# Two convolution layers with weights made per position: pairs of positions as a 128-row stationary operand, the weights of four outputs in one moving pass, and the small networks moved beside the statistics

## The chip, the cores and the metric

The kernel runs on one core of one Trainium2 chip. The metric is the device time of one execution in microseconds (us). Every time below is a median of several executions on the chip, measured in turns with the kernel before on the same chip; a profiled execution of the same kernel is read beside it. One core gives no neighbours on its die to compare with; all profiled runs told here were classed as fast.

## The reference, cut to what matters

The input x has 32 samples (S), 32 batch entries (B), 64 channels (C) and 256 positions (L), all fp32. Two layers of the same form follow each other:

```python
h  = relu(ln(z @ W1 + b1))                        # per (b, l): 16 -> 128
w  = (h @ W2 + b2).reshape(B, L, CI, CO, K)       # own 64 x 64 x 3 weights for every (b, l)
hb = relu(ln(z @ Wb1 + bb1)); bias = hb @ Wb2 + bb2
x_uf = stack of x shifted by -1, 0, +1            # K = 3 taps along l
out  = einsum('sbilk,bliok->sbol', x_uf, w) + bias
x = x + conv(group_norm(x))                       # 32 groups of 8 positions
```

So every position of every batch entry has its own three 64 x 64 matrices, made by a matmul from 128 hidden values, and used for 32 samples only. Making the weights costs more TensorE time than using them.

## The kernel before

Both kernels go through 64 steps (32 batch entries, two layers) of two chunks. In a chunk the weights of 128 positions are made into an SBUF tile `wall` (through PSUM and VectorE, which adds the bias b2); then the convolution of the chunk before is done from `wall`. In the kernel before, the upper and the lower 64 partitions hold the two halves of the positions, so the stationary operands of the weight matmuls are 64 columns wide, and two of them stand in the array side by side (those of the convolution are 64 rows by 32 columns):

```python
def make_weights(t, w2, hT, c, kk, tick):          # once per tap kk
    for o0 in range(0, C, OG):                     # 8 groups of 8 outputs
        pg = ps_g.tile([P, OG, NP], FP, tag="pg", name="pg")
        for o in range(OG):
            for r in range(2):                     # the two halves of the positions
                nc.tensor.matmul(pg[r*C : r*C+C, o, :], w2[k][:, o0+o, :], h[:, r, :, c, :], ...)
        nc.vector.tensor_tensor(wall[...], pg..., b2..., ALU.add)
        tick()                                     # one piece of prepare(b + 1)

def convolve(xn, c):                               # K = 64 rows, two row halves x four column quarters
    for m in range(-1, LC + 1):
        ...
        nc.tensor.matmul(pc[r][q][t*S : (t+1)*S, ...], xn[r*C : (r+1)*C, t*LT + c*LC + m + 1, :], moved(...), ...)

def prepare(par, t, b, res):                       # the small networks of the next batch entry,
    for net in ("w", "b"):                         # spread over the groups of make_weights
        ... matmul, ScalarE, matmul (mean), ScalarE, matmul (variance), ScalarE ...
        nc.vector.reciprocal(sd, sd)               # L255
        nc.vector.tensor_tensor(hc, hc, sd, ALU.mult)   # L256
```

## Time and profile before

The time before was 6762.27 us (median of 3 runs, 6744.58 to 6773.44).

| | before |
|---|---|
| span of the profiled run | 6806.9 us |
| first dense weight matmuls | 412 us |
| one step of the loop | 99.7 us |
| TensorE stops at instruction fetches | 979 us |
| granted clock in the loop | 0.87 |

The prediction shows the main lines. Three more of the page of the kernel before are of use: the granted clock in 40 slices (tenths of full speed), the queue that moves instructions (packets, megabytes, share of the engines' time), and the chain that ended last by engine.

```profile
PEclk9999888898888888898888888888888888988888
...
q8 instruction: 1096, 17.96, 1.3%
...
PE 65%; issue 15%; DVE 8%; DMA 7%; SPq 5%; ACT 1%; POOL 0%; DVEq 0%; POOLq 0%; ACTq 0%
```

The clock stays below full speed all through the loop, and 15% of the chain is "issue", that is TensorE waiting for nothing that the profile shows, which the prediction reads as instruction fetches.

Two stretches of the same kernel, the statistics stage and the loop of layer 0, by engine: length, busy time (and instructions) of PE, PEld, DVE, ACT and POOL, then the clock, the DMA share and GB/s.

```profile
60.00:400.00 340.00, 15.17 (x26) 4.80 (x26) 174.52 (x493) 8.34 (x16) 9.54 (x7) 1.00 0.90 195
520.00:3440.00 2920.00, 2106.19 (x64262) 1931.26 (x64266) 1475.92 (x1994) 148.37 (x326) 810.85 (x208) 0.87 0.59 88
```

In the statistics stage TensorE and ScalarE are nearly empty, and the DMA engines are at 90%. That room is what the change wants to use.

### The profile page before, as it was taken

What the parts mean: (1) busy time and instruction counts of PE and PEld (TensorE: products, weight loads), DVE (VectorE), ACT (ScalarE), POOL (GpSimd) and SP (SyncE); (2) the same over time, 40 slices, a digit from 0 to 9 for tenths busy, and PEclk for the clock granted to TensorE, in tenths of its full rate; (3) what the DMA queues carried; (4) which work ended last, traced back from release to release, by engine and by line L of the source; (5) the groups of instructions that cost most, each with busy time, mean ns of one, the idle gap of its engine ahead of it and who ended that gap; (6) DMA issues with size and microseconds to landing.
All of it is one profiled execution on the core that took longest, in us unless ns stands there. A gap on an engine that the chain in (4) does not pass through costs nothing.

```text
span 6806.9 us, 289596 instructions
## 1 busy us (share of the span) xinstructions
PE 4626.3 (68%) x140322; PEld 4231.2 (62%) x140322; DVE 3263.5 (48%) x4649; ACT 332.3 (5%) x725; POOL 1735.7 (25%) x462
## 2 busy tenths in 40 slices
PE   0057767777766777676677667767776676777667
PEld 0046666666666766676666666766666666766666
DVE  4455445454544555454455444445444444545444
ACT  0000000000000000000001000000000000000000
POOL 0033322322322232233203322223223223222320
PEclk9999888898888888898888888888888888988888
DMA  9947565565656546655745655655654655656564
GB/s 193 226 84 110 76 102 87 77 92 90 93 74 102 88 74 95 90 90 76 102 86 87 109 83 82 95 84 87 88 93 71 96 90 76 91 91 93 71 101 54
DMA packets 2651853, 637.58 MB, mean 94 GB/s; under 512 B 2122240, under 2 KB 2647872, under 8 KB 2647872
## 3 DMA queue, kind: packets, MB, share of 16 engines
q1 hardware_dynamic: 2650688, 619.05, 59.2%
q8 instruction: 1096, 17.96, 1.3%
q14 instruction: 69, 0.57, 0.0%
HBM read 350.53 MB, written 268.44 MB: 91 GB/s over the span
## 4 chain that ended last, share of the span: by engine, by line
PE 65%; issue 15%; DVE 8%; DMA 7%; SPq 5%; ACT 1%; POOL 0%; DVEq 0%; POOLq 0%; ACTq 0%
PE pg L340 47%; PE pc L367 13%; SPq L330 5%; DMA xs<-in_x_dram 4%; DVE hc L256 3%; DVE hsd L255 3%; DMA zt<-in_L_conv_z_dram 2%; PE p L242 2%; PE p L250 1%; PE p L236 1%; DVE wall L343 1%; DMA w<-in_L_conv_W_dram 1%; PE p L265 1%; ACT hTb L259 1%; DVE y L382 0%
## 5 line engine op out<-in xcount | busy, mean ns | idle before, releaser
L340 PE MATMUL pg<-hTw,w 128*64 128x64 f32 x98304 | 3440.0, 236 | 651.7 <-issue 527.0
L340 PEld LDWEIGHTS pg<-hTw,w 128*64 128x64 f32 x98304 | 3307.4, 151 | 872.6 <-issue 686.3
L343 DVE TENSOR_TENSOR wall<-pg,b 128x512 f32<-128x512 f32 x3072 | 2104.0, 690 | 2282.8 <-PE pg L340 2277.5
L367 PE MATMUL pc<-wall,xn 64*32 64x192 f32 (+2 forms) x40960 | 898.0, 314 | 452.7 <-issue 451.5
L367 PEld LDWEIGHTS pc<-wall,xn 64*32 64x32 f32 x40960 | 772.8, 113 | 561.8 <-issue 526.1
L305 POOL TENSOR_TENSOR xn<-xt,gmean 128x4096 f32<-128x4096 f32 x64 | 474.1, 7408 | 2434.8 <-PE pc L367 2270.7
L382 DVE TENSOR_TENSOR y<-pc,y 128x512 f32<-128x512 f32 x512 | 339.7, 684 | 993.8 <-PE pc L367 990.2
L313 POOL TENSOR_TENSOR xt<-xt,bias 128x4096 f32<-128x4096 f32 x64 | 524.5, 8195 | 1096.5 <-ACT bias L267 1096.5
L305 POOL TENSOR_TENSOR xn<-xn,rstd 128x4096 f32<-128x4096 f32 x64 | 663.7, 10371 | 5.0
L236 PE MATMUL p<-zt,W 16*128 16x256 f32 x128 | 55.6, 520 | 399.4 <-DMA zt<-in_L_conv_z_dram 398.1
L236 PEld LDWEIGHTS p<-zt,W 16*128 16x128 f32 x128 | 23.3, 225 | 406.5 <-issue 400.7
L169 DVE BATCH_NORM_STATS2 parts<-xs 128x6 f32<-128x256 f32 x512 | 168.6, 408 | 197.5 <-DMA xs<-in_x_dram 150.2
L256 DVE TENSOR_TENSOR hc<-hc,hsd 128x256 f32<-128x256 f32 x128 | 251.4, 1964 | 4.4
L175 PE MATMUL am_ps<-am,quarter 128*128 128x32 f32 x2 | 0.6, 411 | 371.8 <-DVE am L126 371.8
L238 ACT ACTIVATE hh<-p,b 128x256 f32<-128x256 f32 x64 | 30.3, 474 | 4379.7 <-PE p L236 4379.7
L293 POOL MEMSET xt<- 64x32 f32 x64 | 9.7, 151 | 878.3 <-DMA xb<-xt 878.3
L175 PEld LDWEIGHTS am_ps<-am,quarter 128*128 128x128 f32 x2 | 0.5, 313 | 371.8 <-DVE am L126 371.8
L255 DVE RECIPROCAL hsd<-hsd 128x256 f32<-128x256 f32 x128 | 223.0, 1743 | 14.2 <-ACT hsd L252 14.2
L265 PE MATMUL p<-hTb,Wb 128*64 128x128 f32 x256 | 40.8, 414 | 242.5 <-ACT hTb L259 242.5
L384 DVE BATCH_NORM_STATS2 between<-y 128x6 f32<-128x512 f32 x256 | 177.8, 694 | 8.7
L265 PEld LDWEIGHTS p<-hTb,Wb 128*64 128x64 f32 x256 | 17.4, 187 | 252.5 <-ACT hTb L259 252.5
L242 PE MATMUL p<-hh,center 128*128 128x256 f32 x256 | 115.1, 540 | 2.3 <-ACT hh L238 2.3
(60 smaller groups left out, 673.6 us busy)
## 6 DMA issues: line engine op xcount, KB each, us to landing
xb<-xt SPq DMA_DIRECT2D x128, 1024.0 KB, 10.9
y<-xb SPq DMA_DIRECT2D x512, 256.0 KB, 6.4
xt<-in_x_dram SPq DMA_DIRECT2D x64, 1032.0 KB, 14.4
xt<-x SPq DMA_DIRECT2D x64, 1032.0 KB, 14.4
xs<-in_x_dram SPq DMA_DIRECT2D x64, 1024.0 KB, 40.1
x<-y SPq DMA_DIRECT2D x256, 256.0 KB, 8.0
out_dram<-y SPq DMA_DIRECT2D x256, 256.0 KB, 7.9
w<-in_L_conv_W_dram SPq DMA_DIRECT2D x6, 2048.0 KB, 24.7
```

What stands on the lines that cost most here:

```text
L169: nc.vector.bn_stats(parts[:, g, 2 * q + h, :], t[:, :, g * E : (g + 1) * E])
L242: nc.tensor.matmul(p2, center, h, start=True, stop=True)
L255: nc.vector.reciprocal(sd, sd)
L256: nc.vector.tensor_tensor(hc, hc, sd, ALU.mult)
L305: nc.gpsimd.tensor_tensor(o, i, st[:, :, 1 : GH + 1, None].to_broadcast(shape), op)
L313: nc.gpsimd.tensor_tensor(i, i, bias[:, None, :].to_broadcast([P, S, H]), ALU.add)
L330: nc.sync.dma_start(out=to[:, b, :, l0 : l0 + LT], in_=y[t * S : (t + 1) * S, r])
L340: nc.tensor.matmul(pg[r * C : r * C + C, o, :], w2[k][:, o0 + o, :], h[:, r, :, c, :], start=True, stop=True)
L343: nc.vector.tensor_tensor(wall[:, kk + c, :, o0 : o0 + OG], pg.rearrange("p o l -> p l o"), t["b2"][:, k, None, o0 : o0 + OG].to_broadcast ...
L367: nc.tensor.matmul(pc[r][q][t * S : (t + 1) * S, n0 - q * E : n1 - q * E, :], xn[r * C : (r + 1) * C, t * LT + c * LC + m + 1, :], moved(r ...
L382: nc.vector.tensor_tensor(part, pc[r][q].rearrange("p n o -> p o n"), part, ALU.add)
L384: nc.vector.bn_stats(between[:, r, g, b, :], part)
```

## The change

The intent is to need fewer TensorE instructions in the loop and to take the small networks out of it. Positions are handled in pairs (2p, 2p+1), so the 128 rows of the convolution's stationary operand are 64 channels at two neighbouring positions, and the weights of up to four neighbouring output positions (4 x 64 = 256 columns) move past it. Three kinds of weight groups feed this: kinds 0 and 1 make two taps at once with a 128-column stationary operand, kind 2 makes the two outer taps with two 64-column operands. The small networks run for two batch entries at a time beside the first statistics, and their results wait in DRAM (`hd`, `bd`) until a step loads them. The core of the diff:

```diff
-        for o in range(OG):
-            for r in range(2):
-                nc.tensor.matmul(pg[r * C : r * C + C, o, :], w2[k][:, o0 + o, :], h[:, r, :, c, :], ...)
+            for k in range(OG):
+                w = w2[:, og * OG + k, :]
+                if kind == 0:
+                    nc.tensor.matmul(pg[:, k, :], w[:, C : K * C], even, start=True, stop=True)
+                elif kind == 1:
+                    nc.tensor.matmul(pg[:, k, :], w[:, 0 : 2 * C], odd, start=True, stop=True)
+                else:
+                    nc.tensor.matmul(pg[0:C, k, :], w[:, 2 * C : K * C], odd, start=True, stop=True)
+                    nc.tensor.matmul(pg[C:P, k, :], w[:, 0:C], even, start=True, stop=True)
 ...
-                    for r in range(2):
-                        nc.tensor.matmul(pc[r][q][...], xn[r * C : (r + 1) * C, ...], moved(r, t, c, m, n0, n1), ...)
+                        nc.tensor.matmul(pc[t * S : (t + 1) * S, ...], xn[c][:, t, p + 1, :],
+                                         wall[:, t, a : a + (n1 - n0) * C], ...)
 ...
-    def prepare(par, t, b, res):            # in the loop
+    def hidden(stage, zts, small, i):       # beside first_stats, results to hd[i], bd[i]
 ...
+        def load_pairs(u):
+            src = (x[:, u] if u < B else x1[u - B]).rearrange("s c l -> c s l")
+            nc.sync.dma_start(out=xt[0:C], in_=src)
+            nc.sync.dma_start(out=xt[C:P, :, 0 : L - 1], in_=src[:, :, 1:L])
 ...
+        def after(u, c):                    # after the convolution of (u, c)
+            if u + 1 < U and u + 1 != B:
+                normalize(c)
+            if c == NCH - 1:
+                store(u)
+                ...
+                if u + 2 < U:
+                    load_pairs(u + 2)
+                    load_residual(u + 2)
+                    add_bias(u + 2)         # four pieces through one buffer
 ...
+        order = [(2, og) for og in range(NO)] + [(kind, og) for og in range(NO) for kind in range(2)]
```

## The prediction

> **What bounds the kernel now.** I read the page's busy line first, then the costliest groups, the waits, the chain in order of time, and last the start times of single TensorE records. The main loop has 64 steps (32 batches, two layers), each of two chunks.
>
> ```profile
> PE 4626.3 (68%) x140322; PEld 4231.2 (62%) x140322; DVE 3263.5 (48%) x4649; ACT 332.3 (5%) x725; POOL 1735.7 (25%) x462
> ...
> L340 PE MATMUL pg<-hTw,w 128*64 128x64 f32 x98304 | 3440.0, 236 | 651.7 <-issue 527.0
> ...
> L343 DVE TENSOR_TENSOR wall<-pg,b 128x512 f32<-128x512 f32 x3072 | 2104.0, 690 | 2282.8 <-PE pg L340 2277.5
> L367 PE MATMUL pc<-wall,xn 64*32 64x192 f32 (+2 forms) x40960 | 898.0, 314 | 452.7 <-issue 451.5
> ```
>
> No engine is full. VectorE waits for TensorE (2277.5 us at the weights, 990.2 us at L382), so TensorE's queue sets the pace. An fp32 matmul is two records, each with its weight load: 98304 is twice 128 chunks x 24 groups x 16 matmuls. What stops TensorE is seen in the chain:
>
> ```profile
> 2064.43 3.95 PE pg L340 x128
> 2068.38 0.35 issue
> 2068.72 3.95 PE pg L340 x128
> 2072.67 0.34 issue
> 2073.01 3.95 PE pg L340 x128
> 2076.96 0.34 issue
> 2077.31 3.95 PE pg L340 x128
> 2081.26 4.46 issue
> ```
>
> Every 128 records (256 instructions counting weight loads) it stops without a wait. The instruction queue moved 17.96 MB in 1096 packets of 16,384 bytes; 17.96 MB over 280,644 TensorE instructions is 64 bytes each, and a packet is 256. So these are instruction fetches. In the DMA records a packet takes 1.3 us on average, and TensorE resumes some 1.4 us after it landed. The two "issue" sums, 527.0 + 451.5 = 979 us, are 0.9 us a fetch.
>
> Second, the small networks sit in TensorE's queue and wait for ScalarE and VectorE:
>
> ```profile
> 400.43 0.54 DVE L256 TENSOR_TENSOR hc<-hc,hsd 128x256 f32<-128x256 f32 x1
> 404.39 1.75 DVE L255 RECIPROCAL hsd<-hsd 128x256 f32<-128x256 f32 x1 [3.43 <-ACT hsd L252]
> 406.18 5.17 DVE L256 TENSOR_TENSOR hc<-hc,hsd 128x256 f32<-128x256 f32 x1
> ```
>
> The same multiplication took 0.54 us and, beside a GpSimd operation, 5.17 us. Third, the granted clock is 0.87 in the main loop: these idle stretches cost clock too.
>
> The dense pace is read from the first groups:
>
> ```profile
> 418.73 0.69 DVE L343 TENSOR_TENSOR wall<-pg,b 128x512 f32<-128x512 f32 x1 [0.24 <-PE pg L340]
> 419.66 0.69 DVE L343 TENSOR_TENSOR wall<-pg,b 128x512 f32<-128x512 f32 x1 [0.24 <-PE pg L340]
> 420.59 0.69 DVE L343 TENSOR_TENSOR wall<-pg,b 128x512 f32<-128x512 f32 x1 [0.24 <-PE pg L340]
> ```
>
> A group of 16 matmuls takes 0.93 us: 32 records, two column halves at once, so 58.4 ns per pass of each half. In dense convolution stretches a record takes 20 ns (16 per 0.32 us): 192 columns x 0.83 ns / 8 array tiles. Per step: 48 x 0.93 + 2 x 320 x 0.020 = 57 us. The stretch from 520 to 3440 us holds 64262 records at 2194 a step, so a step lasts 99.7 us. Over 40 us per step are small networks, stops and half clock.
>
> **What the Trainium skill says.** "TensorE: Matmul & The Clock Gate", section "LDWEIGHTS (loading the stationary operand)", gives columns / 1.2 ns whatever the rows. The trace agrees: at L242 (128 stationary columns) the second load starts 107 ns after the first, at L340 (64 columns) 54 ns. At L242 the second matmul starts 320 ns after the first, 107 + 213: a load overlaps the preceding matmul, and 256 moving columns take 213 ns a pass. Same page, "Part 1: The HAM clock gate": half or full clock, decided over windows of 3413 ns. The clock records are 0.5 or 1.0 in multiples of 3.413 us. I summed the array work per window (columns x 0.83 ns x share of the array): all 1309 windows with at least 0.40 of a full array were followed by full clock, all 432 below 0.30 by half; between, about half each. "SBUF — State Buffer", "Who interferes with whom", says a VectorE instruction with two SBUF inputs contends with GpSimd; 0.54 against 5.17 us fits.
>
> **The change, part by part**, per chunk (half a step).
>
> Weights, full-width kinds 0 and 1: 8 groups x 16 matmuls, 128 stationary columns, 64 moving. The moving side takes 53 ns, but the load 107 ns, and a full-width load has no other column half to run beside. With the 5 ns by which 58.4 exceeds 53.3, a pass is 112 ns: 256 x 0.112 = 28.6 us. Before, 16 of the 24 groups made these for 14.9 us. The halved matmul count does not pay; the weight load becomes the bound.
>
> Kind 2 (two half-width matmuls, as before): 4 groups x 32 matmuls x 2 passes x 58.4 / 2 = 7.5 us. Weights together: 36.1 against 22.4 us.
>
> Convolution: 4 quarters x 4 tiles x 1024 columns x 2 passes x 0.833 / 4 column tiles = 6.8 us against 6.4. A quarter of the streamed blocks are zeros, and the row halves no longer run as two tiles.
>
> Fetches: 352 matmuls x 4 = 1408 instructions, 5.5 fetches against 8.5. In kinds 0 and 1, 256 instructions last 14 us; the fetch starts some 100 instructions ahead (1.4 us before the stop, median, at 14.6 ns each), 5.6 us there, which covers it. The two in kind 2 at 1.0 and 1.5 in the convolution at 0.5 us leave 2.8 us against 7.6.
>
> VectorE: 16 operations of 1024 elements at 157 + 1024 x 1.04 = 1.22 us (0.69 for 512, scaled), 19.5 us, plus 4 x 0.68 and, in layer 0, 4 x 0.69: 25 us. It lies under TensorE except after a convolution, where kind 2 needs 2.44 us of VectorE for 1.87 of TensorE and three buffers: about 0.8 us of wait. Changes of shape, some 0.25 us each (seen at 2087): 0.8 us.
>
> Sum: 28.6 + 7.5 + 6.8 + 2.8 + 0.8 + 0.8 = 47.3 us a chunk, x 128 = 6055 us. Before: 49.9.
>
> Small networks beside the statistics: L255 and L256 (474 us of VectorE) and TensorE's waits leave the loop. The statistics stage: 512 x 0.41 = 209 us, 32 hidden blocks x 1.4 = 45, merges about 40, first loads 25, a tail of 10: some 330 us to the first dense weights, against 412. It becomes VectorE-bound, because 4 MB in one piece should beat the 209 GB/s of today's loads. Layer change and end: 35 us. Total 6055 + 330 + 35 = 6420 us. The base holds no half clock; I leave it there because unforeseen savings (shorter stops) and losses look equal in the middle, and put the half clock in the tail.
>
> GpSimd per step: 16 x 1.3 + 28 x 0.34 + 4 x 2.3 = 40 us (2 ns an element over 0.28, from L313 and L306), hidden. Transfers: 10.1 MB a step, but in pieces of 256 B to 4 KB for 128 to 516 B. The chain normalisation, pair load, residual, four bias pieces, next hidden block is about 70 us of the 85 available.
>
> **Rivals.** (1) Half clock. Kinds 0 and 1 fill 53/112 = 0.48 of a window, above the 0.40 seen to suffice, but a stop that drops it would be self-sustaining: at half clock L242's loads lie 164 ns apart, so the work is 0.32, where 23 of 27 half-clock windows stayed half. If it catches one chunk in eight, +15 us each, 6660; if always, some 8300. For: the thin margin. Against: nothing waits within that stretch. (2) Load and matmul do not overlap in a full-width stream: 160 ns a pass, 59.6 us a chunk, 8000 us. Against: L242's 320 ns. (3) The in-order DMA queue becomes the bound: hidden blocks stand behind four bias pieces through one buffer, each waiting for GpSimd. At 20 us late a step, +1280 us, 7700. Against: the 15 us of slack and half as many pieces. (4) Fetches hide altogether: 2.8 us less a chunk, 6060.
>
> **Range and chances.** The two sides nearly cancel in the loop (47.3 against 49.9), so 2 us a chunk, 256 us, decides. Base within some 300 us; (1) at one eighth of the chunks or more has perhaps 0.15, (2) and (3) together 0.1, (4) 0.1. So 6420 us, 6050 to 7150, faster by over 2% (below 6627) 0.68, within 0.12, slower 0.20.
>
> **What would show it.** Kinds 0 and 1: VectorE's full-height evacuations every 3.6 us, 112 ns between passes; 5.1 us would be (2), under 2.5 us my load argument wrong. Granted clock above 0.95 in the loop, and no fetch stops in kinds 0 and 1; a clock near 0.7 would be (1). A wait of the weight matmuls on the hidden block's DMA would be (3). First dense weights at about 330 us. TensorE records 90,000, fetches about 720.

## The result, and the profile after

The changed kernel took 6834.9 us (median of 4 runs, 6814.48 to 6852.78) where the kernel before took 6767.15 us (4 runs). Ratios here and below are the mean time of one kernel's fast runs over that of the other's of the same rounds, so not quite the ratio of the medians: 1.0105, with a 95% interval of 1.0068 to 1.0143. By the 2% criterion that is the same. 6420 us and a gain had been predicted.

The lines of the page of the changed kernel that answer to those of before: busy time, clock, instruction queue, chain, and four costly groups (busy time and mean of one in ns; then idle time before them).

```profile
PE 6225.5 (91%) x91016; PEld 5820.7 (85%) x91016; DVE 3272.1 (48%) x3512; ACT 191.6 (3%) x757; POOL 2455.1 (36%) x3082
...
PEclk7567999999898889999999998999999899999999
...
q8 instruction: 713, 11.68, 0.8%
...
PE 86%; issue 5%; DVE 4%; DMA 2%; ACT 2%; POOL 1%; SPq 1%; ACTq 0%; DVEq 0%; POOLq 0%
...
L400 DVE TENSOR_TENSOR wall<-pg,b 64x1024 f32<-64x1024 f32 (+1 forms) x2048 | 2503.7, 1223 | 2345.3 <-PE pg L385 1215.2
L383 PE MATMUL pg<-hT,w2t 128*128 128x64 f32 x16384 | 2005.9, 283 | 24.0 <-DVE wall L400 15.8
...
L416 PE MATMUL pc<-wall,xn 128*32 128x192 f32 (+2 forms) x24576 | 1022.8, 325 | 240.1 <-issue 212.3
```

TensorE went from 140322 records to 91016, and yet its busy time rose from 4626 to 6226 us. It is now the bound in earnest: 91% busy, and idle "issue" time is down from 15% to 5% of the chain. Fewer instructions and fewer fetches (713 packets for 1096) came as intended; what remained of the work is longer. In the first four slices the clock is at 0.5 to 0.7, where the kernel before had 0.9.

The statistics stage and the loop of layer 0, in the same columns as before:

```profile
60.00:460.00 400.00, 261.83 (x841) 182.86 (x841) 218.79 (x622) 175.14 (x706) 0.00 (x0) 0.57 0.50 186
520.00:3440.00 2920.00, 2719.98 (x40485) 2572.49 (x40478) 1436.32 (x1381) 0.00 (x0) 1114.41 (x1390) 0.92 0.59 107
```

In the stage no engine is full: VectorE works 219 of 400 us, the transfers no longer fill the engines (0.50), and TensorE runs at half clock.

In the loop, kinds 0 and 1 are as dense as predicted. The chain in order of time (start, length, what) in a quiet stretch:

```profile
2925.92 3.57 PE pg L385 x32
2929.50 3.57 PE pg L383 x32
2933.07 3.57 PE pg L385 x32
2936.64 3.57 PE pg L383 x32
```

A pass is one TensorE record, and an fp32 matmul is two. 32 passes take 3.57 us, 111.6 ns each, with no stop in hundreds of instructions. Elsewhere the same groups take twice as long:

```profile
1840.85 3.36 issue
...
1847.04 7.02 PE pg L383 x32
1854.06 6.83 PE pg L385 x32
1860.89 6.83 PE pg L383 x32
```

A stop of 3.36 us in kind 2 dropped the clock to half at 1843.4 us, and it stayed there for 61.4 us, until the chunk's full-width groups were over: 6.83 us for 32 passes is 213 ns each. Seven spells of 51 to 65 us like this one, after stops of 1.1 to 4.8 us, hold nearly all the slow passes of kinds 0 and 1. And the convolution stops for long stretches at a time when blocks of x are being loaded. First the chain, then SyncE's queue of DMA issues (start, length of the issue, what) in the same stretch:

```profile
3092.08 4.79 PE pc L416 x104
3096.87 3.35 issue
3100.21 2.77 PE pc L416 x24
```

```profile
3070.06 0.60 SPq L114 DMA_DIRECT2D xt<-in_x_dram  x1
3070.71 2.76 SPq L115 DMA_DIRECT2D xt<-in_x_dram  x1
3073.59 28.80 SPq L338 DMA_DIRECT2D ys<-in_x_dram  x4
```

The pair load is issued at 3070 us and the residual pieces until 3102 us; the stop of 3.35 us at 3096.87 us lies in between, at the end of the pair load (its second half lands 24.9 us after its issue) and beside the residual pieces.

From the start times of all TensorE records, sorted by kind, the loop splits like this (us in all, 128 chunks). A stop is a long gap between two starts.

| | predicted | after | of it: stops | passes at half clock |
|---|---|---|---|---|
| statistics stage, to the first dense weights | 330 | 472 | | |
| kinds 0 and 1 | 28.6 x 128 = 3661 | 3857 | 4 | 1749 of 32768 |
| kind 2, with its fetch stops and waits | (7.5 + 2.0 + 0.8) x 128 = 1318 | 1215 | 189 | 1865 of 32768 |
| convolution, with its fetch stops and changes of shape | (6.8 + 0.75 + 0.8) x 128 = 1069 | 1273 | 308 | 2182 of 24576 |

The 0.75 is one and a half fetches at 0.5 us. Of the 308 us of stops in the convolution, 46 are two waits at the start of the loop and at the change of layer, 235 are 73 fetch stops of 3.2 us each, and the rest are short gaps at half clock. Of the 189 us in kind 2, some 120 are fetch stops (the page's "issue" at its two lines, 66.8 and 51.3 us); the rest are short waits where the shape changes or VectorE is late. The loop, change of layer included, is 6346 us where 6055 was predicted. With the stage 142 us late, and 17 us after the loop where 35 had been allowed for end and change of layer, that is the whole error of 415 us.

### The profile page after: what moved, and what is told of

Its sections match the earlier page's. It is cut to its first block, busy times and chain, and to the rows that moved or that the text cites. A ratio compares the mean times of both kernels' runs of the same rounds, so it can differ in the third digit from the quotient of the medians.

```text
span 6835.0 us, 194215 instructions
## 1 busy us (share of the span) xinstructions
PE 6225.5 (91%) x91016; PEld 5820.7 (85%) x91016; DVE 3272.1 (48%) x3512; ACT 191.6 (3%) x757; POOL 2455.1 (36%) x3082
## 4 chain that ended last, share of the span: by engine, by line
PE 86%; issue 5%; DVE 4%; DMA 2%; ACT 2%; POOL 1%; SPq 1%; ACTq 0%; DVEq 0%; POOLq 0%
PE pg L383 28%; PE pg L385 28%; PE pc L416 15%; PE pg L387 10%; PE pg L388 3%; DVE wall L400 2%; PE p L166 2%; ACT junk L152 1%; PE p L147 1%; DMA hd<-ht 1%; DVE hs L157 1%; POOL xn L374 0%; DVE ys L426 0%; DMA xt<-in_x_dram 0%; DVE between L428 0%
## 5 line engine op out<-in xcount | busy, mean ns | idle before, releaser
L400 DVE TENSOR_TENSOR wall<-pg,b 64x1024 f32<-64x1024 f32 (+1 forms) x2048 | 2503.7, 1223 | 2345.3 <-PE pg L385 1215.2
L383 PE MATMUL pg<-hT,w2t 128*128 128x64 f32 x16384 | 2005.9, 283 | 24.0 <-DVE wall L400 15.8
L385 PE MATMUL pg<-hT,w2t 128*128 128x64 f32 x16384 | 2005.3, 283 | 0.0
L383 PEld LDWEIGHTS pg<-hT,w2t 128*128 128x128 f32 x16384 | 1958.0, 199 | 36.2 <-PE pg L388 27.5
L385 PEld LDWEIGHTS pg<-hT,w2t 128*128 128x128 f32 x16384 | 1962.6, 200 | 0.0
L352 POOL TENSOR_TENSOR ys<-ys,bt 128x1024 f32<-128x1024 f32 x256 | 602.2, 2353 | 3448.6 <-DMA bt<-bd 2990.2
L416 PE MATMUL pc<-wall,xn 128*32 128x192 f32 (+2 forms) x24576 | 1022.8, 325 | 240.1 <-issue 212.3
L416 PEld LDWEIGHTS pc<-wall,xn 128*32 128x32 f32 x24576 | 742.3, 115 | 507.9 <-issue 250.6
L387 PE MATMUL pg<-hT,w2t 128*64 128x64 f32 x16384 | 1078.6, 228 | 76.8 <-issue 66.8
L388 PE MATMUL pg<-hT,w2t 128*64 128x64 f32 x16384 | 1079.2, 228 | 51.5 <-issue 51.3
L374 POOL TENSOR_TENSOR xn<-xt,gmean 128x32 f32<-128x32 f32 (+1 forms) x1408 | 1024.8, 728 | 262.5 <-PE pc L416 211.9
L387 PEld LDWEIGHTS pg<-hT,w2t 128*64 128x64 f32 x16384 | 1027.6, 143 | 103.1 <-issue 73.8
L388 PEld LDWEIGHTS pg<-hT,w2t 128*64 128x64 f32 x16384 | 1028.2, 143 | 64.6 <-issue 64.3
L374 POOL TENSOR_TENSOR xn<-xn,rstd 128x32 f32<-128x32 f32 (+1 forms) x1408 | 879.5, 625 | 111.7 <-ACT rstd L317 1.5
## 6 DMA issues: line engine op xcount, KB each, us to landing
xt<-in_x_dram SPq DMA_DIRECT2D x32, 2048.0 KB, 14.5
ys<-x SPq DMA_DIRECT2D x128, 512.0 KB, 14.5
xt<-in_x_dram SPq DMA_DIRECT2D x32, 2040.0 KB, 24.9
```

The source lines that it names most:

```text
L352: nc.gpsimd.tensor_tensor(y[:, oq, :], y[:, oq, :], bt, ALU.add)
L374: nc.gpsimd.tensor_tensor(o, i, b, op)
L383: nc.tensor.matmul(pg[:, k, :], w[:, C : K * C], even, start=True, stop=True)
L385: nc.tensor.matmul(pg[:, k, :], w[:, 0 : 2 * C], odd, start=True, stop=True)
L387: nc.tensor.matmul(pg[0:C, k, :], w[:, 2 * C : K * C], odd, start=True, stop=True)
L388: nc.tensor.matmul(pg[C:P, k, :], w[:, 0:C], even, start=True, stop=True)
```

## The experiments

Fifteen kernels ran on the chip after the change, in four groups; those of one group shared the runs of the kernel before. Each is an edit of the changed kernel. All gave correct results except four, which leave out or freeze transfers. The theory at the start: kinds 0 and 1 lose by their weight load (112 ns for what two half-width passes side by side do in 58.4 ns); the loop of normalisation, pair load and bias pieces stands close behind TensorE; the half clock is kept alive by the full-width groups themselves; and the fetch stops are long where transfers run. The rivals are named in each expectation.

| run | us, median | ratio to before, 95% interval |
|---|---|---|
| the change | 6834.9 | 1.0105 (1.0068 to 1.0143) |
| half | 6626.65 | 0.9755 (0.9720 to 0.9791) |
| unchain | 6656.16 | 0.9747 (0.9665 to 0.9828) |
| half_unchain | 6015.66 | 0.8860 (0.8827 to 0.8892) |
| pre | 6812.13 | 1.0010 (0.9945 to 1.0075) |
| mix_unchain | 6245.7 | 0.9201 (0.9184 to 0.9218) |
| quiet (wrong) | 4770.14 | 0.7029 (0.7015 to 0.7044) |
| hybrid | 5963.37 | 0.8786 (0.8765 to 0.8807) |
| half_mix_pre2 | 5860.7 | 0.8631 (0.8603 to 0.8659) |
| mix_only | 6689.18 | 0.9838 (0.9798 to 0.9878) |
| hybrid_mix | 6023.68 | 0.8847 (0.8819 to 0.8875) |
| hybrid_mix_al | 6017.49 | 0.8848 (0.8824 to 0.8871) |
| half_mix_al | 5887.53 | 0.8645 (0.8608 to 0.8682) |
| after_quiet (wrong) | 6237.67 | 0.9180 (0.9145 to 0.9215) |
| after_nopairs (wrong) | 6252.96 | 0.9205 (0.9185 to 0.9224) |
| after_nobias (wrong) | 6680.2 | 0.9827 (0.9793 to 0.9860) |

### half: kinds 0 and 1 at half width

```diff
-   nc.tensor.matmul(pg[:, k, :], w[:, C : K * C], even, ...)
+   nc.tensor.matmul(pg[0:C, k, :], w[:, C : 2 * C], even, ...)
+   nc.tensor.matmul(pg[C:P, k, :], w[:, 2 * C : K * C], even, ...)
```

and the same for kind 1 with `odd`.

> One edit to the changed kernel: in kinds 0 and 1 each full-width matmul is two half-width ones into the two column halves, same weights, same outputs. Theory (the full-width weight load binds, 112 ns a pass): a group falls from 3.6 to 1.9 us, the 28.7 us of kinds 0 and 1 to about 15 us a chunk, so TensorE alone would need about 37 us a chunk and the run would last about 5250 us. Second theory, to be told apart by the same run (a loop of GpSimd and the DMA queue lies just beneath: two normalisations 30 us, pair and residual loads 32, four bias pieces 32 = 94 to 97 us a step in the trace of the changed kernel, against 99 on TensorE): the step stops at 95 us, the run lasts about 6600 us, and TensorE now waits for the hidden block or for the normalised input. If the load does not bind: no change or slower (more instructions), 6800 us or more.

It took 6627 us. Among the waits of this kernel a new one stands out (engine, line, what it waited for: us in all, times, longest):

```profile
PE pg L389 <- DMA hT<-hd: 628.0, 63, 21.4
```

TensorE now waits 10 us a step for the next hidden block, which stands in SyncE's queue behind four bias pieces that pass through one buffer. The step is 95.9 us (loop 6140 us over 64 steps). That is the second of the two expectations. In the changed kernel the pair loads follow each other at 93 to 97 us in most steps, but TensorE's own steps there are as long, so this interval does not say which of the two sets it, and TensorE waited for the hidden block only once, for 1.8 us; its mean step of 99.2 us (6346 over 64) comes from a few steps of 112 to 127 us. What shows the second bound is half itself: with some 1600 us less for TensorE to do (4648 us busy for 6226), the step shrank only to 95.9 us, some 3 us a step. So the weights alone could not show their gain.

### unchain: the bias pieces and the hidden block elsewhere

```diff
-   bp = ctx.enter_context(tc.tile_pool(name="bias", bufs=1))
+   bp = ctx.enter_context(tc.tile_pool(name="bias", bufs=2))
     normalize(c)
+    if c == 0 and 1 <= u and u + 1 < U:
+        add_bias(u + 1)
 ...
                     load_residual(u + 2)
-                    add_bias(u + 2)
 ...
-   if c == 1 and u + 1 < U:
+   if c == 0 and u + 1 < U:
         hs[u + 1] = load_hidden(u + 1)
```

> Full-width weights as in the changed kernel; only the loop of GpSimd and the DMA queue is shortened: the bias of the next step is added after the first normalisation instead of before it, with two bias buffers, and the hidden block is loaded one chunk earlier. If TensorE binds alone: same as the changed kernel, 6835 us within 1.5 percent, though the fetch stops may move since the transfers move. If the loop already held TensorE back: faster by 2 percent or more.

It took 6656 us. The gain is not that of a wait for the queue, for the changed kernel hardly had one: the loads fall into another part of the step, and the convolution went from 1273 to 973 us. Kinds 0 and 1 gave 197 us back: 3515 of their passes ran at half clock for 1749 before (4054 for 3857 us). Four of the long slow spells followed stops in kind 2, and eleven followed stops of 0.9 to 3.2 us within the first 50 passes of the full-width stretch: the fetches there are not covered in every place of the loads.

### half_unchain: both

> Both edits. If the weight load binds first and the loop second: about 75 to 80 us a step (TensorE 37 to 40 us a chunk with 7.5 fetches in place of 5.5, the loop about 70), 5300 to 5650 us, and VectorE at over 60 percent. If the loop was no bound: same as the half-width run alone.

It took 6016 us, a gain of 11% over the kernel before, but not the 5300 to 5650 that the dense pace promised. Kinds 0 and 1 held 456 stops of 2.3 us, 1033 us in all: at half width a group has twice the matmuls, so twice the instructions in half the time, and the fetches that full-width groups cover stand bare again. A loop of 5526 us less all its stops would be some 4200 us.

### pre: the statistics stage in another order

```diff
-   for r in list(running):
+   for r in running[-1:] + running[:-1]:
 ...
-   ht = stage.tile([P, 2, BLK], FP, tag="ht", name="ht")
+   hw = stage.tile([P, BLK], FP, tag="hw", name="hw", bufs=2)
+   hb = stage.tile([P, BLK], FP, tag="hb", name="hb")
```

> Only the statistics stage is edited: each step issues the newest block's first matmuls before the older blocks' later stages, and the hidden block's output has two buffers. Theory (the small networks made a round trip of TensorE, ScalarE and VectorE in order, 12.6 us a step, at half clock, plus waits for the store of the hidden block): first weight matmul at about 340 us instead of 472, run about 6705 us. If VectorE's own work or the x transfers bind the stage: 440 us or later, run within 0.5 percent of the changed kernel.

The first dense weights came at 446 us instead of 472, and the time was 6812 us: the same as the kernel before. The 340 us of the theory were missed; the other branch (440 us or later) came true in its number, but the chain of the stage names neither VectorE's own work nor the transfers of x. A new wait took the old one's place (the same columns as above):

```profile
PE p L147 <- DMA zt<-in_L_conv_z_dram: 130.1, 25, 36.8
```

The load of the next block's `z` stands in SyncE's queue behind a store that waits for ScalarE. An edit called pre2 below also creates the new block, and so issues this load, before it goes on with the older ones. With it the first dense weights come at 416 to 420 us in five kernels, and the wait for `z` is still there (127 us in hybrid, where a block takes 11.2 us), so what bounds the stage then was not settled. In the changed kernel the stage is a round trip of 12.6 us per hidden block through TensorE, ScalarE, VectorE, TensorE, ScalarE and a store, 32 times; by line, 24% of its chain is the transposes, 20% ScalarE's squares, 18% the first matmul and 15% the store.

### mix_unchain: half-width groups between full-width ones

```diff
-   order = [(2, og) for og in range(NO)] + [(kind, og) for og in range(NO) for kind in range(2)]
+   order = [(kind, og) for og in range(NO) for kind in (2, 0, 1)]
```

together with unchain.

> Full-width weights and the shortened loop as in the run before it; only the order of the groups changes: one half-width group of kind 2 before each pair of full-width ones, in place of all four of kind 2 first. Theory (a stop of 1 to 4 us drops the clock for a window of 3.4 us, and in the full-width stretch it stays down for 48 to 61 us, since a half-clock full-width pass of 214 ns does 0.25 of an array's work; it cost 3515 passes x 102 ns = 358 us in the shortened-loop run): the half-width groups lift the work of a window and free the clock within some 15 us, half-clock passes of kinds 0 and 1 fall from 3515 to below 1200, run about 6350 to 6450 us. If the half clock came from something else than too little work: no change, 6656 us within 2 percent.

It took 6246 us, better than expected. The busy line, clock and convolution of this kernel:

```profile
PE 5968.1 (96%) x91016; PEld 5555.5 (89%) x91016; DVE 3271.3 (52%) x3512; ACT 191.3 (3%) x757; POOL 2454.1 (39%) x3082
...
PEclk7559999999999999999998999999999999999999
...
L416 PE MATMUL pc<-wall,xn 128*32 128x64 f32 (+2 forms) x24576 | 923.5, 310 | 31.0 <-DVE ys L426 22.4
```

TensorE is full, and the clock with it. Only 2 passes of kinds 0 and 1 ran at half clock, kind 2 has 6 us of stops in all, and the convolution waits for fetches so little that "issue" is no longer its main wait. The loop is 5756 us, 45.0 us a chunk. What was not expected is that the stops in kind 2 went too. A likely reason, not tested alone, is that its 128 instructions now always have a full-width group before and after them, which gives the next fetch time.

### mix_only: the order alone

> The changed kernel with only the order of the weight groups altered: each half-width group (kind 2) stands between full-width ones, the bias loads stay where they were. If the 178 us of half-clock passes in kinds 0 and 1 and the 370 us of kind-2 stops are the whole of what the order mends, they go and the convolution's stops of about 280 us stay: 6835 - 178 - 370 = some 6290, range 6250 to 6450 us, under 200 half-clock passes in kinds 0 and 1. If the new place of the bias loads had the larger share of what the two did together (6246), it is 6500 to 6700 us.

It took 6689 us, so the first of the two expectations was a miss; the second holds in its range, but the place of the bias loads alone (unchain) gave hardly more: alone the edits are worth some 150 and 180 us, together 589. Kind 2 fell as expected, from 1215 to 1061 us, and the half-clock passes of kinds 0 and 1 to 567. But the convolution went up to 1335 us, with 275 us in 71 fetch stops of 3.9 us. The two edits are not a sum: with the loads where they are, the convolution pays; with the loads moved and the old order, kinds 0 and 1 pay at half clock; only both together leave nobody to pay. It also tests the half clock: with as many long stops as in the changed kernel, the slow passes fell to a third. A half-width group now comes round every 9.0 us (1.9 + 2 x 3.57), where before 28.7 us of full-width groups kept the clock down. Most slow spells are then short (53 under 8 us, 13 longer).

### quiet: half_unchain without the loads of x

```diff
-   load_pairs(u + 2)
-   load_residual(u + 2)
+   pass
```

> Wrong results on purpose: the run with half-width weights and the shortened loop, but pair and residual blocks are loaded for the first two steps only (6 of the 10 MB of a step less). It asks whether the fetch stops (some 1.3 ms in the half-width run, 2.3 us each in kinds 0 and 1) are made long by the block transfers. If transfers make them long: stops at most half, about 5300 to 5500 us. If a fetch simply takes longer than 256 instructions' lead whatever else moves: within 3 percent of 6016 us.

It took 4770 us, 1246 us less than half_unchain on the same TensorE instructions, and less than the 5300 to 5500 us expected. The stops in kinds 0 and 1 fell from 1033 to 293 us, and their passes at half clock from 11340 to 1205. The profile of half_unchain puts these stops down to "issue" and not to data. So the loads of x do not cost by what waits for their data: they make the instruction fetches late.

### after_quiet, after_nopairs and after_nobias: which load

The same question for the changed kernel itself: both loads left out; only the pair loads (4 MB a step) left out; only the bias pieces read once and reused.

```diff
 after_quiet:     -   load_pairs(u + 2)
                  -   load_residual(u + 2)
                  +   pass
 after_nopairs:   -   load_pairs(u + 2)
 after_nobias:    -   bt = bp.tile(...)                     # and its four loads, in every piece
                  +   bt = held[0]                          # loaded once
```

> Wrong result on purpose: the changed kernel without the pair and residual loads from the third step on. If these transfers make the fetches long, the convolution falls from 9.95 to 7.1-7.8 us a chunk and the kind-2 stops from 185 us to under 100, the single long stops that drop the clock go with them: 6835 - 280 - 90 - 150 = some 6300 us, range 6200 to 6450. If the stops belong to the fetches themselves, 6750 to 6850 us.

> Wrong result on purpose: only the pair loads (4 MB a step) left out, the residual pieces (2 MB a step) stay. If the pair loads do it, nearly the time without both, 6250 to 6500 us; if the residual loads do, near the changed kernel, 6700 to 6850 us.

> Wrong result on purpose: the bias pieces are read once and reused, all other transfers stay. If the bias pieces only delay the chain of normalisation, pair load and residual to the moment of the convolution, then without them the loads come at another moment, as when the bias loads were moved: convolution 7.1-8 us a chunk, and 6550 to 6750 us. If the convolution's stops don't depend on them, 6800 to 6850 us.

They took 6238, 6253 and 6680 us. Without the pair loads alone nearly the whole gain is there. The convolution and one half of kind 2 in after_nopairs:

```profile
L387 PE MATMUL pg<-hT,w2t 128*64 128x64 f32 x16384 | 1029.8, 224 | 22.6 <-issue 12.0
...
L416 PE MATMUL pc<-wall,xn 128*32 128x64 f32 (+2 forms) x24576 | 920.5, 309 | 30.1 <-DVE ys L426 29.0
```

The convolution lost its "issue" wait of 212 us. Against the changed kernel the loop is shorter by 578 us (5768 for 6346): 312 in the convolution, 136 in kind 2, 130 in kinds 0 and 1, which have 489 passes at half clock instead of 1749. In the changed kernel the fetch stops of the convolution are 3.2 us each; here none is left. In kind 2 the "issue" wait is 12 us; its 186 other gaps, of 0.3 to 0.5 us, are not fetches: 124 stand at the change to kind 0 (the first full-width load waits for the last half-width matmul, or the group for VectorE), and 62 before kind 2's last group. The trace of the changed kernel says how the stops become so long: the fetch itself takes about as long in both places (1.51 us in the convolution, 1.43 in kind 2, medians of the stops over 0.5 us), but it starts later: in the convolution a median of 0.4 us after TensorE has stopped, in a tenth of them over 1.5 us after, and in kind 2 a median of 1.3 us before the stop. TensorE resumes 1.5 to 1.6 us after the packet has landed in either case.

That it is the pair loads alone does not follow, since leaving them out also moved the residual pieces. With the DMA records of a trace each fetch can be sorted by what the DMA engines moved from 4 us before it started until it had landed. In the convolution of the changed kernel, 76 of 91 fetches beside loads of x stopped TensorE (236 us in all), and 1 of the 98 others. In kind 2, 74 of 89 fetches beside the residual pieces alone stopped it, by 1.3 us on average. In after_nopairs none of the 187 fetches of the convolution and one of 161 in kind 2 fell beside residual pieces; 112 fell in kinds 0 and 1, and stopped nothing. In half_unchain, kinds 0 and 1, 153 of 181 fetches beside the pair load stopped TensorE (3.5 us on average), 132 of 166 beside the stores of the result (1.5 us), and 27 of 135 beside neither these nor residual pieces (0.2 us). So in these traces the stops stand beside large transfers, the longest beside the loads of x. That is a coincidence in time; what quiet and after_nopairs add is that the stops go when the loads of x, or the pair loads with the old place of the residual pieces, are taken away.

after_nobias fell in its range, but not for the reason expected: its convolution takes 9.4 us a chunk and not 7.1 to 8, and still has 198 us of fetch stops. The bias traffic itself matters little.

On why a fetch starts late, the Trainium skill, "DMA: Bandwidth & Descriptors", section "Queues, rings and completion order", says that an engine serves its queues in turn and finishes a whole packet of one, typically 9 to 17 descriptors, before it goes to the next. The rows of the pair load took 88.6 to 97.7 ns each in the DMA records, so a packet of them would hold an engine for some 0.8 to 1.7 us: this is an estimate from the page and those durations, of the right size for the delay. No run here shows it as the cause.

### hybrid, half_mix_pre2 and hybrid_mix: how much of the width to give back

hybrid makes kind 1 alone half-width, with unchain and pre2, in the old order. half_mix_pre2 makes all kinds half-width, in the new order. hybrid_mix is hybrid in the new order.

> Kind 0 full-width, kind 1 as two half-width matmuls, alternating; shortened loop; statistics stage with the newest block's input loaded and its matmuls issued first. Theory (a full-width group gives the next instruction fetch 3.6 us of cover, at a work share of 0.63 so that no half clock sticks): a pair of groups takes 5.5 to 6.0 us against 7.1 (full) and 6.0 with stops (half), stops in kinds 0 and 1 under 400 us in all, run 5750 to 5950 us; first weight matmul at about 380 us instead of 472. If the cover does not help: 6050 us or more.

> All half-width, shortened loop, kind 2 spread between the others, same statistics stage as the hybrid run. Against 6016 us of the half-width run with the shortened loop: minus about 90 us from the stage, and about 1 us a chunk less waiting for VectorE after a convolution: 5800 to 5930 us. If the stage stays at 440 to 470 us: about 5950 us.

> Kind 1 half-width as well, kind 0 full-width, the three kinds in turn, with the moved bias loads and the reordered statistics stage. If the fetch stops are covered by the full-width group that stands in every three and nothing is lost to half clock: per chunk 14.3 (kind 0) + 7.5 + 7.5 (kinds 1 and 2) + 7.1 (convolution) + 2 to 4 us of stops = 38.5 to 40.5 us, times 128, plus 416 and 20: 5350 to 5620 us. If two half-width groups in a row (256 matmuls' worth of fetches in 3.7 us) leave the stops as long as they were, it is no better than the hybrid in the old order, 5860 to 5960 us.

hybrid took 5963 us, just over its range, with the first weights at 416 us and not 380. Its stops in kinds 0 and 1 are 213 us, as expected, but 2862 passes of these kinds (602 of them full-width) ran at half clock, in 15 spells of over 8 us and some 60 short ones. half_mix_pre2 took 5861 us, the fastest correct kernel here, 13.7% below the kernel before. Its busy line:

```profile
PE 4518.9 (77%) x123784; PEld 4101.5 (70%) x123784; DVE 3251.6 (55%) x3512; ACT 191.5 (3%) x757; POOL 2462.6 (42%) x3082
```

TensorE has 1700 us less to do than in the changed kernel and is idle again for a quarter of the time: its fetch stops sum to some 1190 us. hybrid_mix was a miss: 6024 us, no better than hybrid. In its loop of 5587 us the stops are some 160 us in the convolution, 200 in kind 1 and 97 in kind 2, and 753 passes of kind 0 ran at half clock. One full-width group in three did not cover the fetches of two half-width ones, as two in three did those of one in mix_unchain. Sorted as above, 100 of the 135 fetches of kinds 1 and 2 beside the pair load stopped TensorE, and 21 of the 125 others; in the convolution 70 of 84 beside residual pieces did.

### hybrid_mix_al and half_mix_al: whole rows in the second pair load

```diff
-   nc.sync.dma_start(out=xt[C:P, :, 0 : L - 1], in_=src[:, :, 1:L])   # 1020-byte rows from 4 bytes in
+   nc.sync.dma_start(out=xup, in_=src)        # whole 1024-byte rows, to a place one element lower
```

> As the run before it, but the second pair load reads whole 1024-byte rows to a place one element lower, in place of 1020-byte rows that begin 4 bytes in (24.9 us against 14.5 us for the other half's whole rows). If the short rows cost the transfer its time, the load lands in about 14.5 us and the fetch stops near it become fewer: 50 to 200 us less than without. If it is only the second in a queue of two and shares the engines with the residual pieces, 22 to 27 us as before, and the time within 30 us.

> All kinds half-width, in turn, with every other edit and the whole rows. Without the whole rows it took 5861 us, with stops of 596 + 417 + 211 us. If the short rows prolong the fetches that meet the load, 5650 to 5800 us; if not, 5830 to 5890 us. All half-width and faster than the one-in-three full-width kernel would say that a full-width group covers nothing.

The second load had landed 24.9 us after its issue in the changed kernel, the first 14.5. The landing of that load (least, median, most) in hybrid_mix_al, with whole rows:

```profile
DMA to landing us min/median/max: 24.1/24.6/25.4
```

In hybrid_mix, with the short rows, it was 24.0, 25.0 and 25.7 us. The row itself took less time (89.8 ns for all rows, where the short ones had taken 97.7), but neither the landing nor the time changed: 6017 against 6024 us, and 5888 against 5861 us. The second load is simply second: 4 MB in 24.6 us. The Trainium skill, "DMA: Bandwidth & Descriptors", section "Rules for kernel authors", says that two transfers to separate halves of the partitions share the same engines and so follow each other; the trace agrees.

## Why the prediction was wrong

No gain came where one of 5% was forecast. The prices of the weight passes and of VectorE were right. Three terms failed: the cost of a fetch in the convolution (0.5 us allowed, 3.2 us a stop measured), the half clock that the base left out (178 us), and the statistics stage (330 us allowed, 472 measured). By its own steps:

**Pass of 112 ns, "the weight load becomes the bound": right.** 111.6 ns. The price shows where it is not paid: TensorE's busy time falls by 1700 us in half_mix_pre2, where all kinds are half-width (the half clock that the changed kernel lost is in that difference too, so it is not the weight load alone). The step from 22.4 to 36.1 us of weights a chunk was rightly seen.

**"16 operations of 1024 elements at 1.22 us", under TensorE: right.** 1223 ns, and VectorE waits for TensorE 2345 us in L400.

**"Fetches about 720", "TensorE records 90,000": right**, 713 and 91016. "The fetch starts some 100 instructions ahead, which covers it" in kinds 0 and 1: right as well, 3 stops in 32768 passes.

**"The two in kind 2 at 1.0 and 1.5 in the convolution at 0.5 us": the term that failed, in the convolution.** No reason is given for the 1.0 and 0.5, and the prediction's own lines say otherwise: L367's 451.5 us over its 320 fetches are 1.4 us each in the convolution, L340's 527.0 us over 768 are 0.7 us each in the weights. Nor is it one number: without the pair loads hardly any fetch stops TensorE in either place; with them there are 73 stops of 3.2 us in the convolution, 235 us where 0.75 x 128 = 96 was allowed, and some 120 us in kind 2, where 2.0 x 128 = 256 was. Half clock after the stops (2182 passes at 73.5 ns for 37.2, short gaps included, some 79 us) and the 46 us of waits at the start and at the change of layer are the other part of the 204, less what the dense pace saved (7.08 us a chunk for 7.6, 66 us). The prediction compared the transfers (10.1 MB a step) with the queue's time, and never asked what they do to the fetches. after_nopairs shows the size: 582 us by the medians, 312 us of the loop's part in the convolution; that run also moved the residual pieces.

**"The base holds no half clock; I leave it there because unforeseen savings and losses look equal in the middle": wrong, and rival (1) was the right mechanism at the wrong size.** "Nothing waits within that stretch" was true and beside the point: the stops before the stretch drop the clock. A pass at half clock took 214 ns, twice its 112 at full clock, and not the 164 ns of the rival. So its array work is 53.3/214 = 0.25 of a window and not 0.32, far in the range in which the clock stays down: all of some 115 half-clock windows with work from 0.20 to 0.255 stayed half. The 1749 passes cost 1749 x 102 ns = 178 us of the 196 by which kinds 0 and 1 were over. In the number of chunks it was less than the rival's one in eight (1749 of 32768 is one in nineteen), at nearly twice the price (256 x 102 ns = 26 us more for a chunk that runs slow throughout, for 15). mix_unchain tested it: with half-width groups in between and the loads moved, 2 slow passes were left.

**"Some 330 us to the first dense weights", "it becomes VectorE-bound": wrong.** 472 us, and VectorE busy for 219 of 400 us. The stage is bound by a round trip of the small networks, 32 x 12.6 = 403 us. The prediction had counted 45 us of VectorE for them and no waiting. "4 MB in one piece should beat the 209 GB/s" was also not seen: 186 GB/s over the stage, because the loads now wait for the stage and not the reverse. pre brought 26 us of it and pre2 some 55, so the order of the work was only part.

**Rival (3), "against: the 15 us of slack": the slack was some 3 us.** The queue was not the bound of the changed kernel, but its chain, put at about 70 us a step, takes some 95: half stopped at 95.9 us a step against the 99.2 of the changed kernel.

**The sum.** Too low by 142 us in the stage, 196 in kinds 0 and 1 and 204 in the convolution, too high by 103 in kind 2, which is luck: its fetches and its waits for VectorE had both been put too high. The prediction's view that "the two sides nearly cancel in the loop" was right; it then put 0.68 on one side of a difference of 2.6 us a chunk, whose largest unknowns (clock and fetch delay) both had one sign.

What stays open: by which mechanism the transfers delay a fetch, how much of it is due to the pair loads and how much to the residual pieces, and what bounds the statistics stage after pre2.

## What to carry to other kernels

Price an instruction-fetch stop by where it falls beside the loads, not by its mean: here the means ranged from nothing to some 4 us, and moving a load or putting a slow, instruction-poor group next to a dense one was worth as much as the arithmetic. A stream whose array work at half clock lies under the level that brings the clock back (here 0.25 of a window) must be broken up by denser work, or one stop costs the whole stream twice its time. And before a bound is removed, measure the period of the second one: a chain of loads through single buffers stood some 3 us of 99 beneath.

## What the Trainium skill lacked or had wrong

- "Runtime: NRT & Kernel Launch", section "Instruction fetch mechanics", gives blocks of 16 KiB and 256 instructions, which the trace confirms (packets of 16,384 bytes, stops every 128 records with their loads). It says that the fetch is hidden by the time that instructions take to issue. Here it is not: 979 us of stops in the kernel before, by fetches that start a median of 1.4 us before the stop.
- No page says that large transfers delay instruction fetches, though the turns of the queues cited above would let one expect it: in the convolution of the changed kernel 76 of 91 fetches beside loads of x stopped TensorE and 1 of 98 others, and without the pair loads the loop is 578 us shorter.
- "TensorE: Matmul & The Clock Gate", "Part 1: The HAM clock gate", speaks of idle and busy windows. A window can be in between, and the state then lasts: from 0.20 to 0.255 of the array's work all of some 115 half-clock windows stayed half (seven spells of 51 to 65 us after stops of 1.1 to 4.8 us), while all but 3 windows with 0.40 or more were followed by full clock.
- The same page, "LDWEIGHTS (loading the stationary operand)": the load time of columns / 1.2 ns holds for full clock (112 ns a pass); at half clock the pass took 214 ns. Whether the load itself slows or no longer overlaps the matmul there, no run here separates.
- "DMA: Bandwidth & Descriptors", section "How a descriptor splits into AXI transactions", has no measured time for rows that do not start aligned: rows of 1020 bytes from 4 bytes in took 97.7 ns, for 88.6 ns of whole rows in the same kernel, but a 2 MB load of them landed no later (25.0 against 24.6 us).
